# A new order of operations in a five-stage software pipeline of graph layers

## Chip, cores and metric

The kernel runs on one core of a Trainium2 chip. The metric is device time in microseconds (us), the median of several executions; lower is better. The core has five engines that each work through a queue of their own, in order: PE (TensorE, matrix products), DVE (VectorE), ACT (ScalarE), POOL (GpSimd) and SP (SyncE, which here issues all transfers). An instruction that waits holds up everything behind it on its engine.

## What is computed

64 graphs of 256 nodes with 256 features pass through two layers. Each has an adjacency matrix with values that select among four relations.

```
# layer 0: attention of 8 heads, masked by relation r = 0..3
q, k = x @ Wq + bq, x @ Wk + bk                       # per head, 32 columns each
attn = softmax(q k^T / sqrt(32))
out  = sum over r of (attn * (adj == r)) @ (x @ Wv[r] + bv[r])
x1   = layernorm(x + out @ Wo + bo)
x2   = layernorm(x1 + gelu(x1 @ W1 + b1) @ W2 + b2)
# layer 1: two rounds of graph attention, then a feed-forward
Wh = h @ W; e = leaky_relu(Wh a1 + (Wh a2)^T)
h  = softmax(where(adj > 0, e, NEG), axis=1) @ Wh     # done twice
x3 = layernorm(x2 + h)
x4 = layernorm(x3 + relu(x3 @ w_ff1 + b_ff1) @ w_ff2 + b_ff2)
```

All products are in float32.

## The kernel before

Each graph is one chain of 225 named operations. `Graph.operations` (L687) makes them, and the table `PLACES` (L28) gives each a place in time, as if a new graph began every `PERIOD` = 60 units. The launch loop (L769 to L782) makes a list of all operations of all graphs, graph g's shifted by g x 60, sorts it by place, and calls them in that order. A place therefore has no other effect than the order in which instructions enter the five queues. Places go over more than five periods, so while graph g is at its first products, graphs g-1 to g-5 are at later stages. The sort, and no scheduler, fixes the order:

```python
        for _, _, f in sorted(plan, key=lambda p: p[:2]):
            f()
```

Four further functions are sorted in the same way: `v_weights` (L258), two calls of `ffn_weights` (L232) and `gat_weights` (L262), which prepare weights once, at `V_PLACE`, `FFA_PLACE`, `FFB_PLACE` and `GAT_PLACE`; and some fifty loads of weights from `LOAD_PLACE` on, `LOAD_STEP` apart.

The names, with the engine on which they run (m is 0 or 1, a half of the heads; h is 0 to 3, a head):

- load, cast, jT, xT, mask0 to mask4: SP loads x and adj, POOL makes adj bf16, SP transposes it by a transfer, DVE transposes x, POOL compares adj with each relation.
- qk m (PE), qkc m (ACT): queries and keys into PSUM, then into SBUF. s m (PE): scores of four heads. max, rec (DVE), exp, nrm (ACT): softmax.
- eT (DVE), eW, eR (SP): the weights are transposed in squares of 32, written to DRAM and read back in another layout. ec (ACT) copies them to PSUM, pm (DVE) multiplies them with three masks, pl (POOL) with the fourth.
- xS (DVE), vp1 to vp7 (PE), vc1 (ACT), va1 to va9 (DVE), vb0, vb1 (POOL): values of all relations, by seven block products in place of eight, with their sums and bias.
- po m (PE, 32 products of four heads side by side), oT m (ACT copies it to SBUF), y, yb, wo (PE), ya (DVE): head outputs, output product and residual.
- st, rt, nb, ln (DVE, POOL, POOL, ACT), lg, lb (POOL): layer norms 1 to 4.
- For the two feed-forwards (a with GELU, b with ReLU): aT, aW, aR transpose as above; au0 to au3 (PE) the first product; ax0 to ax3 (ACT) its function; aS1 to aS4 (POOL) and ad1 to ad7 (PE) the second product by seven block products; ae, ae1, ae5, ae6, ae7 (DVE) add them; ag, ar (POOL) prepare the residual. The b operations likewise.
- hT, hW, hR, ga0, ga1 (PE), gac0, gac1 (ACT), then twice ip (PE), z (ACT), zm, zx (DVE), ze (ACT), zd (DVE and ACT), with h10, h11 (PE, copied by h1c0, h1c1 on ACT) after the first round (A) and h2 (PE, added by h2a on DVE) after the second (B): graph attention.
- store (SP): the result.

Buffers matter as much as places. Nearly all products of PE (qk, vp, wo, u0 to u3, po, ga, ip, h1, h2, and d2 to d4 together) take turns in two PSUM banks:

```python
    ps_mm = ctx.enter_context(tc.tile_pool(name="ps_mm", bufs=2, space=bass.MemoryType.PSUM))
```

So a product waits until the product two before it has been read by ACT or DVE. d1, d5, d6 and d7 share one more bank; ec has one bank (tag "pe"), the four score tiles one bank each. In SBUF the transposed squares have three buffers, e and pm and pl four, eT three.

ACT computes a function from a set of tables; where the next function is not in the set at hand, an ACT_TABLE_LOAD stands before it in the built program. Exp (exp, ze) and GELU (ax) need different sets.

Of the kernel before, what the change touches and what calls it, by code (L numbers as in the profile page):

```python
# [25 lines left out]

PERIOD = 60.0
PLACES = {  # L28
    "load": 23.357, "xT": 44.608, "cast": 52.922, "jT": 64.605, "mask0": 69.219, "qk0": 72.09,
    "qkc0": 73.299, "mask1": 76.86, "s0": 78.011, "max02": 87.686, "exp02": 89.264, "qk1": 89.326,  # L30
    "max00": 91.141, "qkc1": 92.707, "exp00": 96.206, "rec02": 99.233, "max03": 99.873, "max01": 100.286,
    "mask2": 100.655, "rec00": 100.829, "nrm02": 101.294, "eT02": 101.781, "nrm00": 102.264, "xS": 102.642,
    "eT00": 102.765, "mask3": 102.981, "exp03": 104.45, "exp01": 105.68, "eW02": 108.309, "rec03": 109.52,
    "vp1": 110.158, "rec01": 110.803, "y": 111.209, "vc1": 113.257, "vp6": 114.571, "s1": 115.506,
    "va6": 115.853, "vp2": 116.039, "eR02": 119.674, "nrm01": 120.359, "max10": 120.437, "va1": 120.827,
    "yb": 121.298, "eW00": 123.019, "exp10": 123.155, "max11": 124.031, "nrm03": 124.245, "rec10": 125.086,
    "nrm10": 125.786, "max13": 129.917, "eR00": 129.963, "exp11": 130.688, "vp7": 131.698, "eT01": 131.873,
    "exp13": 132.201, "va7": 132.519, "vb1": 132.554, "eT10": 133.02, "max12": 133.458, "pl00": 133.78,
    "exp12": 134.344, "vp5": 135.541, "eT03": 136.074, "va9": 137.432, "va5": 137.492, "vp4": 138.406,
    "va4": 138.429, "eW03": 139.955, "ec02": 139.991, "eW01": 140.081, "pm02": 140.771, "eR01": 142.073,  # L40
    "rec12": 143.085, "pl02": 143.665, "rec11": 144.369, "rec13": 144.684, "vp3": 145.914, "ec01": 146.17,
    "nrm13": 147.545, "pm01": 149.231, "va3": 149.974, "nrm11": 150.098, "pl01": 150.355, "ec00": 151.68,
    "eR03": 151.833, "nrm12": 153.205, "mask4": 154.895, "eT13": 154.901, "pm00": 156.208, "ec03": 156.841,
    "vb0": 157.326, "eW10": 158.121, "pl03": 159.226, "eT11": 159.823, "pm03": 159.89, "eW13": 159.97,
    "eW11": 161.977, "po0": 162.822, "eR11": 162.889, "ec11": 163.67, "oT0": 164.697, "eR10": 165.613,
    "eR13": 166.702, "pm11": 167.743, "ec13": 167.832, "eT12": 167.88, "pl11": 170.085, "pm13": 170.45,
    "pl13": 172.693, "eW12": 172.935, "pl10": 173.109, "ec10": 174.083, "eR12": 178.038, "pm10": 178.658,
    "ec12": 179.982, "pm12": 181.436, "pl12": 183.147, "po1": 190.604, "oT1": 190.634, "wo": 195.515,
    "ya": 196.954, "st1": 198.358, "rt1": 200.264, "nb1": 202.568, "ln1": 205.212, "aT": 205.925,
    "aW": 214.402, "aR": 215.033, "au0": 217.723, "ag": 219.066, "ax0": 219.075, "au1": 220.077,  # L50
    "au2": 220.423, "ax1": 220.498, "au3": 221.942, "ax2": 222.429, "ax3": 223.227, "aS1": 224.059,
    "aS3": 226.672, "aS2": 228.949, "ad1": 229.288, "ad5": 232.772, "ad7": 233.221, "ar": 236.067,
    "ad6": 237.512, "aS4": 241.549, "ad2": 244.054, "ae5": 244.725, "ad3": 244.935, "ad4": 246.881,
    "ae1": 248.098, "ae6": 248.952, "ae": 249.383, "ae7": 250.355, "st2": 254.869, "rt2": 255.472,
    "nb2": 255.506, "ln2": 255.669, "lg2": 259.788, "lb2": 259.86, "hT": 261.844, "hW": 265.63,
    "hR": 271.783, "ga0": 272.609, "gac0": 274.207, "ga1": 274.252, "gac1": 274.962, "ipA": 275.589,
    "zA": 275.992, "zmA": 277.16, "zxA": 278.103, "zeA": 278.374, "zdA": 283.105, "h10": 283.502,
    "h11": 286.253, "h1c0": 287.71, "h1c1": 289.589, "ipB": 290.919, "zB": 291.939, "zmB": 292.107,
    "zxB": 294.725, "zeB": 295.859, "zdB": 298.561, "h2": 301.635, "h2a": 303.541, "st3": 304.449,
    "rt3": 304.465, "nb3": 307.95, "ln3": 307.966, "bT": 311.255, "bW": 313.954, "bR": 315.237,  # L60
    "bu0": 319.27, "bx0": 320.506, "bu1": 320.552, "bu2": 322.215, "bx1": 323.13, "bu3": 323.143,
    "bx2": 325.826, "bg": 326.199, "bx3": 327.872, "bd1": 328.16, "bS1": 328.916, "br": 329.424,
    "bd5": 330.387, "bS2": 331.057, "bS4": 331.173, "bS3": 331.831, "bd2": 334.692, "be5": 334.871,
    "bd3": 337.158, "bd4": 337.445, "bd6": 337.996, "be": 338.193, "be1": 338.799, "bd7": 340.197,
    "be6": 343.454, "be7": 346.517, "st4": 346.806, "rt4": 355.06, "nb4": 361.434, "ln4": 362.111,
    "lg4": 364.143, "lb4": 369.218, "store": 370.908,
}
LOAD_PLACE, LOAD_STEP = 62.0, 3.0
V_PLACE, FFA_PLACE, GAT_PLACE, FFB_PLACE = 92.0, 199.0, 202.0, 260.0

# [739 lines left out]
```

## Time and profile before

| what | value |
|---|---|
| median of 3 runs | 3690.38 us (3680.24 to 3691.91) |
| the profiled execution | 3687.13 us, span of its instructions 3685.0 us |
| PE, DVE, ACT, POOL busy | 3497.9, 2880.7, 2628.1, 3019.8 us |
| transfers | 458 MB, mean 124 GB/s, 16 engines 42.1% busy |
| first instruction of PE's first product | 7.84 us after the span's start |

The span is from the first to the last instruction of the profile; what the execution takes beyond it is 2.1 us. The transfers are many and of one kind: per graph 11 squares of 256 KB are written and read again. Page lines on them (issues, size, median us from issue to landing):

```profile
eT_d<-eT_sq SPq DMA_DIRECT2D x512, 256.0 KB, 3.1
eT<-eT_d SPq DMA_DIRECT2D x512, 256.0 KB, 3.1
hT_d<-hT_sq SPq DMA_DIRECT2D x64, 256.0 KB, 3.2
```

In the trace a float32 product is two MATMUL records, so qk, of four products, shows as x8. Names of tiles stand for operations: h_ps L664 is h1, h_ps L678 is h2, ga_wps is ga, ffb_ps and ffa_ps are bu and au, ffa_po, ffa_pq, ffb_po and ffb_pq are ad and bd, v_ps is vp, pe L568 is ec.

### The profile page before, as it was taken

The page shows a single profiled execution, that of the slowest core. Times are in us where ns is not written, and L with a number is a line of the kernel's source. Part 1 is how long each engine was busy: PE and PEld are TensorE (multiplying, and loading weights), DVE is VectorE, ACT ScalarE, POOL GpSimd, SP SyncE. Part 2 cuts the span into 40 slices and gives each one's busy share as a digit, 9 for nine tenths or more (in the row PEclk, how much of TensorE's full clock was granted, in tenths as well). Part 3 has the DMA queues.
Part 4 walks back from the last instruction along what each step waited for, and adds up shares of the span by engine and source line. Part 5 has one row for each costly group of instructions (what it writes and reads, how often), then busy time and mean ns, then how long its engine had stood idle before and what let it go on. Part 6 is the DMA issues. An engine that isn't in the chain of part 4 may idle for free.

```text
span 3685.0 us, 73450 instructions
## 1 busy us (share of the span) xinstructions
PE 3497.9 (95%) x25816; PEld 2749.5 (75%) x25816; DVE 2880.7 (78%) x5208; ACT 2628.1 (71%) x6981; POOL 3019.8 (82%) x3142
## 2 busy tenths in 40 slices
PE   6799999999999999999999999999999999999995
PEld 3577777777777777777777777777777777777775
DVE  5688888878888888778788788788788888788762
ACT  4577777777777777777777777777777777777752
POOL 4588888888888888888888888888888888888864
PEclk8899999999999999999999999999999999999997
DMA  6344444444444444444444443444444444444420
GB/s 180 111 119 124 135 126 124 133 118 124 137 124 123 134 126 123 131 127 122 132 127 124 134 128 121 133 127 123 128 126 124 132 126 123 134 127 123 126 86 26
DMA packets 809889, 457.97 MB, mean 124 GB/s; under 512 B 334256, under 2 KB 718896, under 8 KB 809520
## 3 DMA queue, kind: packets, MB, share of 16 engines
q1 hardware_dynamic: 809520, 453.27, 42.1%
q8 instruction: 204, 3.34, 0.4%
q14 instruction: 165, 1.35, 0.1%
HBM read 243.42 MB, written 201.33 MB: 121 GB/s over the span
## 4 chain that ended last, share of the span: by engine, by line
PE 62%; DVE 17%; ACT 8%; DMA 6%; issue 3%; POOL 2%; SPq 2%; POOLq 0%; ACTq 0%; DVEq 0%
PE ffb_ps L387 10%; PE v_ps L511 9%; PE po L589 5%; PE ffa_po L422 5%; DVE pm L572 4%; PE ffb_pq L422 4%; PE qk_ps L487 4%; PE ffa_ps L387 4%; DVE eT_sq L306 4%; PE ffb_po L422 4%; PE ffa_pq L422 3%; PE ga_wps L619 3%; PE s L537 3%; DVE nmax L542 3%; PE h_ps L678 2%
## 5 line engine op out<-in xcount | busy, mean ns | idle before, releaser
L572 DVE TENSOR_TENSOR pm<-rel,pe 128x1536 f32<-128x1536 uint8 x512 | 891.4, 1741 | 123.4 <-ACT pe L568 110.7
L577 POOL TENSOR_TENSOR pl<-rell,eT 128x512 f32<-128x512 bf16 x512 | 595.9, 1170 | 15.5 <-DMA eT<-eT_d 15.2
L560 ACT ACTIVATE e<-e,rden 128x256 f32<-128x256 f32 x1024 | 463.0, 503 | 145.3 <-DVE rden L555 145.1
L387 PE MATMUL ffa_ps<-ffa_T,w 128*128 128x256 f32 x2048 | 478.2, 382 | 8.9 <-ACT e L550 3.3
L550 ACT ACTIVATE e<-s,nmax 128x256 f32<-128x256 f32 x1024 | 475.5, 475 | 5.6 <-DVE nmax L542 4.6
L387 PE MATMUL ffb_ps<-ffb_T,f 128*128 128x256 f32 x2048 | 458.0, 382 | 20.9 <-DMA ffb_T<-ffb_T_d 20.8
L387 PEld LDWEIGHTS ffb_ps<-ffb_T,f 128*128 128x128 f32 x2048 | 392.4, 192 | 102.9 <-issue 36.2
L387 PEld LDWEIGHTS ffa_ps<-ffa_T,w 128*128 128x128 f32 x2048 | 377.1, 192 | 55.3 <-ACT e L550 5.3
L589 PE MATMUL po<-pm,v 128*32 128x256 f32 x6144 | 363.7, 384 | 19.9 <-DVE pm L572 6.6
L568 ACT COPY pe<-eT 128x512 f32<-128x512 f32 x512 | 306.9, 599 | 87.0 <-ACT gb_wh L659 48.0
L306 DVE STREAM_TRANSPOSE eT_sq<-e 128x512 f32<-128x512 f32 x512 | 354.2, 692 | 14.9 <-DMA eT_d<-eT_sq 9.8
L542 DVE TENSOR_REDUCE nmax<-s 128x2 f32<-128x512 f32 x512 | 342.9, 670 | 5.8 <-PE s L537 5.8
L395 ACT ACTIVATE ffb_h<-ffb_ps,bf_c 128x256 f32<-128x256 f32 x512 | 212.4, 466 | 183.2 <-PE ffb_ps L387 183.2
L520 DVE TENSOR_TENSOR v<-v,v_ps 128x512 f32<-128x512 f32 x448 | 298.7, 678 | 35.0 <-PE v_ps L511 32.5
L430 DVE TENSOR_TENSOR ffb_res<-ffb_po,ffb_res 128x256 f32<-128x256 f32 (+2 forms) x256 | 130.4, 509 | 240.7 <-PE ffb_po L422 134.5
L589 PEld LDWEIGHTS po<-pm,v 128*32 128x32 f32 x6144 | 206.8, 110 | 149.1 <-issue 18.2
L479 POOL TENSOR_SCALAR rel<-adT 128x512 uint8<-128x512 bf16 x192 | 289.7, 1509 | 18.8 <-DMA adT<-adb 17.6
L528 POOL TENSOR_TENSOR v<-v,bv_r 128x512 f32<-128x512 f32 (+1 forms) x128 | 232.5, 1816 | 71.5 <-DVE v L520 71.5
L410 POOL TENSOR_TENSOR ffa_h<-ffa_h,ffa_h 128x512 f32<-128x512 f32 x64 | 82.0, 1281 | 221.9 <-ACT ffa_h L395 217.5
L395 ACT ACTIVATE ffa_h<-ffa_ps,b_c 128x256 f32<-128x256 f32 x512 | 212.2, 465 | 36.0 <-PE ffa_ps L387 35.0
L364 ACT ACTIVATE ffa_res<-ffa_res,nb_x,rs_x 128x256 f32<-128x256 f32 x256 | 139.9, 593 | 135.5 <-POOL nb_x L359 135.5
L550 ACT ACTIVATION_READ_ACCUMULATOR e<-s,nmax 128x1 f32 x1024 | 211.1, 206 | 0.0
(154 smaller groups left out, 8444.7 us busy)
## 6 DMA issues: line engine op xcount, KB each, us to landing
eT_d<-eT_sq SPq DMA_DIRECT2D x512, 256.0 KB, 3.1
eT<-eT_d SPq DMA_DIRECT2D x512, 256.0 KB, 3.1
xin<-in_x_dram SPq DMA_DIRECT2D x256, 64.0 KB, 2.7
adi<-in_adj_dram SPq DMA_DIRECT2D x64, 256.0 KB, 3.3
y<-in_x_dram SPq DMA_DIRECT2D x64, 256.0 KB, 4.6
ffa_T_d<-ffa_T_sq SPq DMA_DIRECT2D x64, 256.0 KB, 3.5
ffa_T<-ffa_T_d SPq DMA_DIRECT2D x64, 256.0 KB, 2.9
hT_d<-hT_sq SPq DMA_DIRECT2D x64, 256.0 KB, 3.2
```

Source lines behind the costliest of these rows:

```text
L306: nc.vector.transpose(self.sq.rearrange("p a c k y -> p (c k) a y"), src.rearrange("p c (k a x) -> p (c k) a x", k=KD, a=A))
L387: nc.tensor.matmul(p[:, f - f0, :], self.wa[:, k, f * P:(f + 1) * P], self.x.nodes(k), start=(k == 0), stop=(k == KD - 1))
L395: nc.scalar.activation(self.h[half][:, f1 + f, :], self.ps[f0][:, f, :], self.func, bias=self.ba[:, f0 + f:f0 + f + 1])
L422: nc.tensor.matmul(self.p[bank][:, k], a[:, f], seven[self.name[:3]][i][:, f], start=(f == 0), stop=(f == KF // 2 - 1))
L511: nc.tensor.matmul(self.ps["v", i], a, wv_s[i], start=True, stop=True)
L542: nc.vector.tensor_reduce(self.nmax[m, h], self.s4[m][h].rearrange("p (c n) -> p c n", c=C), AX.X, ALU.max, negate=True)
L550: nc.scalar.activation(e[:, ic, :], self.s4[m][h][:, ic * N:(ic + 1) * N], AF.Exp, bias=self.nmax[m, h][:, ic:ic + 1], accum_out=self.den[ ...
L560: nc.scalar.activation(e[:, ic, :], e[:, ic, :], AF.Copy, scale=self.rden[m, h][:, ic:ic + 1])
L568: nc.scalar.copy(self.pe[m, h], self.et[m, h].t.rearrange("p b c k y -> p (b c k y)"))
L572: nc.vector.tensor_tensor(self.pm[m, h], self.rel.rearrange("p r b c k y -> p r (b c k y)"), bc(self.pe[m, h], [P, R - 1, C * N]), ALU.mult)
L577: nc.gpsimd.tensor_tensor(self.pm_l[m, h], self.rel_l.rearrange("p b c k y -> p (b c k y)"), self.et[m, h].t.rearrange("p b c k y -> p (b ...
L589: nc.tensor.matmul(po[hp, :], self.v[m][:, jc, r, hp], w, start=(r == 0 and jc == 0), stop=(r == R - 1 and jc == C - 1))
```

## The change

Only numbers change: all places in `PLACES`, and the places of the weight preparations and weight loads. `PERIOD`, the functions, the instructions' shapes and the pools stay as they are.

```diff
 PERIOD = 60.0
 PLACES = {
-    "load": 23.357, "xT": 44.608, "cast": 52.922, "jT": 64.605, "mask0": 69.219, "qk0": 72.09,
...
-    "lg4": 364.143, "lb4": 369.218, "store": 370.908,
+    "load": -20.281, "cast": 3.418, "xT": 3.616, "jT": 16.208, "qk0": 32.188, "mask0": 32.245,
...
+    "lg4": 344.387, "lb4": 346.024, "store": 352.412,
 }
-LOAD_PLACE, LOAD_STEP = 62.0, 3.0
-V_PLACE, FFA_PLACE, GAT_PLACE, FFB_PLACE = 92.0, 199.0, 202.0, 260.0
+LOAD_PLACE, LOAD_STEP = 20.0, 3.0
+V_PLACE, FFA_PLACE, GAT_PLACE, FFB_PLACE = 50.0, 168.0, 198.0, 235.0
```

What it makes of the queues is seen when all places are taken modulo 60 from qk0 of graph g. A number after the name tells how many graphs back the operation belongs (qk0 is of graph g, bu0-4 of graph g-4). PE's queue over one period before:

```
qk0 wo-2 vp5-1 s0 vp4-1 bu0-4 bu1-4 bu2-4 bu3-4 vp3-1 bd1-4 qk1 bd5-4 ga0-3 ga1-3 bd2-4 ipA-3
bd3-4 bd4-4 au0-2 bd6-4 au1-2 bd7-4 au2-2 au3-2 po0-1 h10-3 h11-3 ad1-2 vp1 ipB-3 ad5-2 ad7-2
vp6 s1 vp2 ad6-2 h2-3 ad2-2 ad3-2 ad4-2 po1-1 vp7
```

and after:

```
qk0 vp5-1 ad5-3 ad2-3 ad6-3 ad4-3 ad3-3 vp4-1 vp2-1 s0 vp3-1 qk1 bu0-4 bu1-4 bu2-4 bu3-4 au0-2
au1-2 bd1-4 po0-1 ga0-3 ga1-3 bd5-4 ipA-3 vp1 bd6-4 vp6 bd2-4 bd4-4 bd3-4 au2-2 bd7-4 h10-3 s1
h11-3 au3-2 ipB-3 ad1-2 po1-1 vp7 wo-1 h2-3 ad7-2
```

After, in the same period, the parts of the other queues that the prediction follows:

```
DVE  st1-2 rec11-1 ae7-3 va9-1 va5-1 ae5-3 bT-4 rec13-1 ae6-3 rec12-1 rec10-1 ae-3 st2-3 va4-1 va1-1
     aT-2 eT11-1 va3-1 pm03-1 eT13-1 max00 max01 pm01-1 hT-3 max03 rec00 pm02-1 eT12-1 max02 xS ...
     pm12-1 max10 max11 max13 eT02 eT03 zmB-3 zxB-3 st4-4 max12 va7 zdB-3 pm00 ya-1 ae1-2 h2a-3 st3-3
ACT  exp12-1 qkc0 ln3-4 exp13-1 ln4-5 nrm11-1 ln1-2 nrm10-1 ec03-1 nrm12-1 nrm13-1 ln2-3 qkc1 bx0-4
     ec01-1 bx1-4 exp00 bx2-4 exp01 bx3-4 ec02-1 ax0-2 nrm00 ax1-2 ec13-1 exp03 oT0-1 gac0-3 gac1-3
     exp02 zA-3 vc1 ec11-1 nrm01 zeA-3 zdA-3 ec10-1 ax2-2 h1c0-3 ec12-1 nrm03 h1c1-3 nrm02 ax3-2
     zB-3 exp11 ec00 oT1-1 zeB-3 zdB-3 exp10
SP   load+1 eR01-1 eW02-1 bW-4 bR-4 aW-2 aR-2 store-5 eR02-1 eW13-1 eW11-1 eR13-1 hW-3 hR-3 eR11-1
     eW12-1 eW10-1 eR10-1 eR12-1 eW00 eR00 jT+1 eW01 y eW03 eR03
```

In the queues before, ACT has ax0 to ax3 with nrm02, nrm00 and zdA between them and no Exp; SP has bW, bR, two eW, eR01, load, then hW and hR next to each other.

## The prediction

> **What bounds the kernel now.** I read the page first (busy shares and slices), then the busy time by windows, then who PE waited for in the middle of the run, then the timeline around PE's one regular wait, and last the chain of waits at both ends.
>
> ```profile
> PE 3497.9 (95%) x25816; PEld 2749.5 (75%) x25816; DVE 2880.7 (78%) x5208; ACT 2628.1 (71%) x6981; POOL 3019.8 (82%) x3142
> PE   6799999999999999999999999999999999999995
> ```
> PE is full from the third slice to the last but one. Only there can an order gain or lose.
>
> ```profile
> 1000.00:1600.00 600.00, 585.56 (x4378) 460.92 (x4377) 488.39 (x887) 445.22 (x1187) 511.93 (x535) 1.00 0.43 127
> 1600.00:2200.00 600.00, 585.14 (x4393) 461.51 (x4392) 487.58 (x886) 443.98 (x1184) 512.21 (x533) 1.00 0.43 127
> ```
> Windows: after the length come the busy times of PE, PEld, DVE, ACT, POOL, then clock and DMA. PE idles 14.7 us in 600, the clock is full, and no other engine is above 86%. Who ends PE's idle time between 1000 and 3400 us (total, times, longest):
>
> ```profile
> PE h_ps L664 <- ACT oT L595: 40.1, 44, 1.4
> PE ga_wps L619 <- DMA hT<-hT_d: 10.1, 12, 2.7
> PE ffa_ps L387 <- DMA ffa_T<-ffa_T_d: 3.2, 4, 1.6
> ```
> So one wait comes in each of the 44 periods, of 0.9 us; the transfer hT adds 10.1/44 = 0.23 us. The timeline shows the first:
>
> ```profile
> 2443.97 0.59 ACT L568 COPY pe<-eT 128x512 f32<-128x512 f32 x1
> 2444.58 1.28 ACT L550 ACT_TABLE_LOAD   x1
> 2445.87 0.48 ACT L550 ACTIVATE e<-s,nmax 128x256 f32<-128x256 f32 x1
> 2446.79 0.37 ACT L595 COPY oT<-po 128x256 f32<-128x256 f32 x1
> 2447.21 1.14 PE L664 MATMUL h_ps<-ga_wh,ga_z 128*128 128x258 f32 x4 [1.21 <-ACT oT L595]
> ```
> h11 needs the second of two PSUM buffers, which oT0 empties. oT0 stands on ACT behind ec11, a table load and exp03. From the chain of waits at both ends:
>
> ```profile
> 203.34 1.73 PE qk_ps L487 x8
> ...
> 3460.07 1.73 PE qk_ps L487 x8
> ```
> These are qk0 of graphs 4 and 63, so a full period is (3460.07-203.34)/59 = 55.2 us; 203.3 us lie ahead and 3685.0-3460.1 = 224.9 behind.
>
> [...] I use start-to-start times. [...] the load starts 0.02 us after ec11's end and exp03 0.01 us after the load, so I charge 1.28 us. [...] Here like transfers of 256 KB land in 2.0 us (ffb_T_d) to 3.5 us (ffa_T_d)[...].
>
> **The change, part by part.** No computation comes or goes; each engine's queue is reordered.
>
> *Table loads.* GELU (ax0 to ax3) and Exp are different sets.
>
> ```profile
> L395 ACT ACT_TABLE_LOAD x64 | 82.1, 1283 | 0.3
> L550 ACT ACT_TABLE_LOAD x62 | 79.5, 1283 | 1.1
> ```
> Before, the four GELUs stand together: one pair of loads a graph. After, the queue reads ax0, ax1, exp03, exp02, zeA, ax2, ax3, exp11: two pairs. The built program has 257 loads for 129, so ACT does 128 x 1.283 = 164 us more and reaches 2792 us, 76%. It costs only where ACT's queue sets PE; checked below.
>
> *PE.* Start-to-start times of before without a wait: 12 products of 1.73 (qk, up-products u, wo, h2) 20.8; 7 vp of 0.86, 6.0; 14 down-products d of 0.89, 12.5; 2 po of 3.59, 7.2; 2 s, 2.2; ga, h1 and ip, 4.1; and 0.1 on each side of each s and po, 0.8. Sum 53.5 us. Before pays 55.2: 1.0 at h11, 0.4 at ga0, 0.3 elsewhere.
>
> Next I laid the new PE queue out back to back, qk0 at 0, and followed what each PE step needs through the other queues, with the trace's steps: DVE 0.60 (pm 1.67), ACT 0.73 for pairs reading PSUM, 0.81 nrm, 0.91 exp, 0.52 ec, 1.0 ln, POOL 1.23 (pl 1.12, mask 1.46), 0.05 a hand-over. The tight places, in order of the period:
>
> 1. vp2 (7.90) takes the bank that ae empties after ad3 (6.15): 6.15+1.05+0.05+0.55+0.05 = 7.85. Free, by nothing. In front of ae stands bT, behind ln3 (ends 3.75), so DVE is there in time (6.0).
> 2. bu0 (12.62) takes vp3's bank, behind ae, st2, va4, va1, aT, eT11, va3: 11.8. Its data: bT ends 4.5, bW and bR 2.2 and 2.7: about 10. Free.
> 3. po0 (23.99) needs pm02: bu3 ends 19.70, bx3 20.5, ec02 21.0, pm02 22.8. pl02 follows vb0 on POOL (18.9+1.1). Free.
> 4. ga1 (28.56) takes po0's bank. ACT from bu3's end: bx3, ec02, load, ax0, nrm00, ax1, ec13, load, exp03 end at 27.3; po0 ends 27.65, oT0 28.1. Both loads are in this chain, with 1.0 us to spare before ga1. This is before's wait: gone, because ga0 and bd1 lie between.
> 5. ga0 (27.58) needs hT. aT ends 10.5; aW 3.5 lands 14.1; SP, which stops at aR until then, issues aR, store, eR02, eW13, eW11 in 2.4 us. eR13 stops SP until eW13 lands, near 20[...]; then hW 3.1, hR 3.8: near 27.2. By the transfers' extremes 26 to 29. Cost -0 to 1.4, and I take 0.3: before loses as much there.
> 6. po1 (44.59) takes au3's bank, 41.65+1.89+0.04+0.82+0.05 = 44.45; ax2's load falls ahead of au3's end. Free by 0.1.
> 7. h2 (50.87) needs zdB. On DVE zdB stands behind va7, which waits for vp7 (48.18): 48.18+1.12+0.04+0.59+1.11+0.05 = 51.1. Cost 0.2. exp11's load is ahead of oT1 (47.2 against po1's end 48.25): hidden.
>
> Everything else (buffers of e, eT, pm, pl, squares) comes free over 0.5 us before a PE step needs it, by the same steps. Waits known: 0.3+0.2. For those my steps don't see, 0.2 (before too has 0.3 elsewhere). New period 54.2 us, gain 1.0.
>
> *SP and POOL.* Same issues, new places: eR00 now follows eW00 at once and stops SP about 3 us, in front of jT and eW01; jT's first reader mask0 comes 12 us after it lands, and eT01 is ready later than the stop ends. store moves ahead of eR02; its operand lb4 is done at 11.5, so it doesn't stop SP, where before it waited for POOL. POOL adds nothing and has some 6 us free a period.
>
> *Ends.* Head: the same first products and the same weights; gat_weights moves from 10 to 46 us into period 2, out of ffn_weights' neighbourhood. I keep 203.3, +-8. Tail: bu0 stands 12.6 instead of 6.4 us after qk0, which delays the last graph's last feed-forward: 225+6 = 231, +-8.
>
> Sum: 203.3 + 59 x 54.2 + 231 = 3632 of span. The profiled execution took 3687.13, 2.1 above its span: 3634. The median shown, 3690.38, is 3.3 above that execution, inside the runs' spread of 11.7; I add 2 of it: 3636, so 438 + 59 x T for every case.
>
> **Rivals.**
>
> *One wait for another (no change).* Places 1, 6 and 7 have 0.2 us or less to spare. If my 0.04 to 0.05 hand-overs are short, as for before, whose h11 wait flips between 0.39 and 1.2, three waits of 0.4 arise on top of the known 0.5: T = 55.0, 438+59x55.0 = 3683. For it: the 0.3 us a period in before that no list names. Against: PE-bound waits in series aren't added, since a later PE step relaxes the next place.
>
> *The burst on SP (slower).* Place 5: ad3 to hT by way of ae, aT, aW, aR, store, eR02, eW13, eR13, hW, hR, five of them stopping SP in turn. PE work between ad3 and ga0 is 21.4 us, the chain 21.0. Before has no such run there: hW goes out at 10.6, hR at 14.0 with nothing between them, hT lands at 17.8 against ga0 at 17.7, and still 0.2 is lost. If transfers in the burst land 0.5 us later each than I took, the chain is 23.5, T = 53.5+2.1+0.4 = 56.0, total 3742. It decides where T passes (3690-438)/59 = 55.1, a chain of 22.6. For it: DMA is busy 43% and y, in a burst, takes 4.6 us. Against: hT's typical 3.8 us is charged already.
>
> *Table loads show (slower).* If ec02 waits for eR02 (lands near 19, needed 20.5) by 2.5 us, place 4 loses 1.5 and po0 1.2: T about 55.6, 3718.
>
> **How the numbers follow.** This kernel's measurement tells 0.3% (11 us) from no change. Forecast (T 53.6 to 54.85): 0.66, from 438+59x53.6 = 3600 to 3674, 3636 likeliest. Waits exchanged: 0.12, 3674 to 3701, of which 0.02 still faster by over 11 us. Burst 0.15, 3701 to 3765. Table loads 0.07, 3701 to 3730. Faster by over 0.3% 0.68, within 0.10, slower 0.22. The range 3592 to 3720 leaves out about 0.12 above and 0.03 below, where head or tail also gain their 8 us.
>
> **What would show it.** PE's wait "h_ps L664 <- ACT oT" vanishes; a wait of "h_ps L678 <- ACT gb_wh" of 0.2 us comes; table loads x128 and near x124 under L395 and L550, 1283 ns each; ACT near 2790 us; start-to-start of qk0 54.2. Wrong if PE waits over 1 us a period at ga_wps for hT, at v_ps for DVE, or at ffb_ps or po for ACT, or if head and tail move by over 15 us.

## The result, and the profile after

The changed kernel takes 3914.07 us (median of 4 runs, 3906.63 to 3951.67), the kernel before in the same comparison 3688.23. The ratio is 1.0636 (95% interval 1.0566 to 1.0706): 226 us slower, where 3636 was forecast, and beyond the range's upper end of 3720. The profiled execution took 3914.44 us, its span is 3912.5 us.

From the page of the changed kernel, busy times and slices:

```profile
PE 3565.3 (91%) x25816; PEld 2758.2 (70%) x25816; DVE 3131.6 (80%) x5208; ACT 2799.4 (72%) x7109; POOL 3012.4 (77%) x3142
PE   5899989999999899998999999899999899999985
```

PE now has holes in the middle of the run. DVE has as many instructions as before and is busy for 251 us more. ACT has 128 instructions more, the table loads, and its 2799 us are near the 2792 of the sum. A window of the changed kernel (busy times of PE, PEld, DVE, ACT, POOL, then clock, DMA share and GB/s):

```profile
1000.00:1600.00 600.00, 558.62 (x4079) 434.42 (x4079) 499.50 (x825) 443.25 (x1130) 478.75 (x498) 0.98 0.41 119
```

PE idles 41.4 us in 600, nearly three times as much as before, and no engine looks full. Who ends its idle time from 1000 to 3400 us (total, times, longest):

```profile
PE ffb_po L422 <- DVE rden L555: 112.3, 41, 5.8
PE v_ps L511 <- DVE ffa_res L430: 40.6, 41, 1.0
PE ga_wps L619 <- DMA hT<-hT_d: 2.6, 4, 1.0
```

Before's wait of h11 (h_ps L664) for oT is gone, as forecast, and the transfer hT costs 2.6/41 = 0.06 us a period. Two new waits came, one each in every period. The second is vp2 waiting for ae, place 1 of the prediction. The first is bd6 (ffb_po), on no list of mine.

From qk0 to qk0 the periods are of two lengths: of 50 in the middle of the run, 30 take 56.2 us and 20 take 63.0 in the mean. The mean from graph 4 to graph 63 is 58.82. Set against the sum:

| part | forecast | traced | difference |
|---|---|---|---|
| head, to qk0 of graph 4 | 203.3 | 198.4 | -4.9 |
| 59 periods | 59 x 54.2 | 59 x 58.82 | +272.6 |
| tail | 231 | 243.7 | +12.7 |
| span | 3632 | 3912.5 | +280 |

So the period is the place to look. Start to start, PE's steps in the new order take what the sum gave them, but for two: from vp4 to vp2 it is 2.1 us instead of 0.86, and from vp1 to bd6 2.2 in the short periods (1.3 lost), 6.8 in the long ones (5.9 lost). Here is PE's timeline in a long period (start, duration, then the idle time ahead and who ended it):

```profile
1234.52 1.02 PE L511 MATMUL v_ps<-wv,xT 128*128 128x512 f32 x2
1241.29 2.05 PE L422 MATMUL ffb_po<-f_t,ffb_t 128*128 128x128 f32 x8 [5.75 <-DVE rden L555]
1243.13 1.91 PE L511 MATMUL v_ps<-wv_t,xs 128*128 128x512 f32 x2
```

After the wait, bd6 takes 1.84 us to the next start and vp6 1.71, where 0.97 and 0.86 are usual, and the granted clock of this stretch and of the next is low (windows of the changed kernel):

```profile
1236.40:1241.50 5.10, 0.21 (x1) 0.24 (x2) 5.10 (x11) 3.21 (x10) 2.12 (x2) 0.67 0.21 70
1241.50:1243.00 1.50, 1.50 (x8) 1.50 (x9) 1.09 (x2) 0.73 (x3) 0.00 (x0) 0.50 1.12 346
```

Around the wait of 1.14 us in a short period the clock stays at 1.00 (1593.00 to 1594.50 and 1594.50 to 1597.00 us), and in the 5.75 us wait it falls to the 0.50 of the second window; from 1245.00 to 1247.00 us it is 1.00 again. From 1000 to 3400 us bd6 takes 2.04 or 2.05 us after each of the 15 waits of 5.32 to 5.76 us, and 1.02 to 1.13 after the 26 of 0.49 to 1.17 us. The slower steps behind it cost about 2.2 us more: the long periods are 6.8 us longer than the short ones, and the longer wait accounts for 4.6 of them (6.8 less 2.2). In the first window DVE is busy all the time, 5.10 of 5.10. Whoever is late is DVE, and it isn't waiting by the look of it. The chain of waits of the changed kernel through this stretch says with what (start, us, what):

```profile
1228.03 8.29 DVE xs L453
...
1240.56 0.59 DVE ffb_res L430
1241.15 0.08 DVE rden L555
...
1241.29 2.05 PE ffb_po L422 x8
```

bd6 waits for be1 (ffb_res L430; the list names rden, which ends last, but the experiment with be1 late shows that it is be1), and be1 stands behind one 128x128 difference of xS that took 8.3 us. In each of the 41 periods between 1000 and 3400 us, short or long, bd6 starts 4.25 us after xS ends: it is late by as much as xS is. DVE's and POOL's timelines of the changed kernel there:

```profile
1227.96 8.36 DVE L453 TENSOR_TENSOR xs<-xT 128x128 f32<-128x128 f32 x1
1236.35 0.29 DVE L453 TENSOR_TENSOR xs<-xT,xs 128x128 f32<-128x128 f32 x1
```

```profile
1227.80 1.29 POOL L410 TENSOR_TENSOR ffb_t<-ffb_h,ffb_t 128x512 f32<-128x512 f32 x1
...
1233.31 2.29 POOL L577 TENSOR_TENSOR pl<-rell,eT 128x512 f32<-128x512 bf16 x2
1235.55 2.97 POOL L479 TENSOR_SCALAR rel<-adT 128x512 uint8<-128x512 bf16 x2
```

Between the first and the last of these POOL works without a gap. The difference is done only when POOL has come to its masks (L479); the next one, beside the masks, takes 0.29. In a short period the same four differences look like this (DVE, then POOL):

```profile
1585.84 1.28 DVE L453 TENSOR_TENSOR xs<-xT 128x128 f32<-128x128 f32 x1
1587.15 1.25 DVE L453 TENSOR_TENSOR xs<-xT,xs 128x128 f32<-128x128 f32 x1
1588.33 1.37 DVE L453 TENSOR_TENSOR xs<-xT 128x128 f32<-128x128 f32 x1
1589.62 0.69 DVE L453 TENSOR_TENSOR xs<-xT,xs 128x128 f32<-128x128 f32 x1
```

```profile
1585.65 1.32 POOL L410 TENSOR_TENSOR ffb_t<-ffb_h,ffb_t 128x512 f32<-128x512 f32 x1
1586.88 1.37 POOL L331 TENSOR_TENSOR ffa_res<-y,g_r 128x512 f32<-128x512 f32 x1
1588.22 1.33 POOL L410 TENSOR_TENSOR ffb_t<-ffb_h,ffb_t 128x512 f32<-128x512 f32 x1
1589.50 0.66 POOL L457 CAST adb<-adi 128x512 bf16<-128x512 int32 x1
```

Each DVE record ends 0.15 us after a POOL record does: 1587.12 and 1586.97, 1588.40 and 1588.25, 1589.70 and 1589.55, 1590.31 and 1590.16. Here DVE gets one difference done at each boundary of POOL's run, in 1.25 to 1.37 us each for the first three. The long one took 8.36, in which six boundaries passed, and in the masks, which read SBUF too, the differences took 0.28 to 0.29. In a period xS is DVE's only TENSOR_TENSOR with both inputs in SBUF: pm, ya, va and the additions take one input from PSUM. zm, a COPY_PREDICATED which reads a mask and a constant column from SBUF, takes 0.76 to 0.78 us in the changed kernel from 1000 to 3400 us, whether POOL works beside it or not.

Before, xS stood where POOL mostly had gaps: of its 176 differences between 1000 and 3400 us, 143 began with POOL idle and took 0.25 to 0.29 us; the other 33 took 0.36 to 1.11. By form, before and then after (busy, mean ns; table loads with it):

```profile
L453 DVE TENSOR_TENSOR xs<-xT 128x128 f32<-128x128 f32 x128 | 64.6, 505 | 0.0
L453 DVE TENSOR_TENSOR xs<-xT,xs 128x128 f32<-128x128 f32 x128 | 36.9, 288 | 2.2
```

```profile
L453 DVE TENSOR_TENSOR xs<-xT 128x128 f32<-128x128 f32 x128 | 300.4, 2347 | 0.0
L395 ACT ACT_TABLE_LOAD x128 | 164.2, 1283 | 62.3 <-PE ffa_ps L387 61.1
L550 ACT ACT_TABLE_LOAD x124 | 159.1, 1283 | 2.2
L453 DVE TENSOR_TENSOR xs<-xT,xs 128x128 f32<-128x128 f32 x128 | 90.2, 705 | 2.2
```

xS goes from 101.5 us in all to 390.6, that is from 1.6 to 6.1 us a graph. The 289 us are more than DVE's whole rise of 251.

The other wait, vp2's, has another cause. DVE's timeline of the changed kernel ahead of it:

```profile
1560.64 0.69 DVE L430 TENSOR_TENSOR ffa_res<-ffa_po,ffa_res 128x512 f32<-128x512 f32 x1 [1.40 <-PE ffa_po L422]
...
1565.89 0.42 DVE L430 TENSOR_TENSOR ffa_res<-ffa_po,ffa_res 128x256 f32<-128x256 f32 x1 [2.05 <-PE ffa_po L422]
...
1569.06 0.56 DVE L430 TENSOR_TENSOR ffa_res<-ffa_pq,ffa_res 128x384 f32<-128x384 f32 x1
```

These are ae1, ae7 and ae of one graph. ae1 adds d1, a product of before po1, but it starts when ad7 ends (1560.53); ae7 adds d7, finished at that same 1560.53, but it starts when ad6 ends (1565.85). d1, d5, d6 and d7 are columns of one tile in one PSUM bank, and each addition here starts 0.11 and 0.04 us after the end of a later product that PE has been given ahead of it on that tile. Likewise bd6 waits for be1, though they touch different columns. No run here tells whether the shared bank or the shared tile makes the program wait. What stands on DVE between ae7 and ae (va9, va5, ae5, bT and others) is held back with it, ae ends at 1569.62, and vp2 follows (PE's timeline of the changed kernel):

```profile
1567.56 1.12 PE L511 MATMUL v_ps<-wv,xs 128*128 128x512 f32 x2
1569.67 1.13 PE L511 MATMUL v_ps<-wv,xT 128*128 128x512 f32 x2 [0.99 <-DVE ffa_res L430]
```

Adding up with weights 0.6 and 0.4 for short and long periods: PE's work 53.5, vp2 1.25, bd6 0.6 x 1.3 + 0.4 x (5.9 + 2.2) = 4.0, ga0 0.1: 58.9, against the traced 58.82.

### The profile page after: what moved, and what is told of

Read it like the earlier page. It is cut to its first block, busy times and chain, and to the rows that moved or that the text cites. A ratio compares the mean times of both kernels' runs of the same rounds, so it can differ in the third digit from the quotient of the medians.

```text
span 3912.5 us, 74077 instructions
## 1 busy us (share of the span) xinstructions
PE 3565.3 (91%) x25816; PEld 2758.2 (70%) x25816; DVE 3131.6 (80%) x5208; ACT 2799.4 (72%) x7109; POOL 3012.4 (77%) x3142
## 4 chain that ended last, share of the span: by engine, by line
PE 71%; DVE 19%; ACT 4%; issue 3%; DMA 2%; SPq 1%; POOL 0%; POOLq 0%; DVEq 0%; ACTq 0%
PE po L589 9%; PE ffb_ps L387 9%; PE ffa_ps L387 9%; PE v_ps L511 8%; PE ffa_po L422 6%; DVE xs L453 5%; PE qk_ps L487 5%; PE ffb_po L422 5%; PE ffb_pq L422 5%; PE s L537 3%; DVE pm L572 3%; PE h_ps L664 3%; PE h_ps L678 3%; DVE ffa_res L430 3%; PE wo_ps L609 3%
## 5 line engine op out<-in xcount | busy, mean ns | idle before, releaser
L387 PEld LDWEIGHTS ffa_ps<-ffa_T,w 128*128 128x128 f32 x2048 | 385.2, 191 | 51.5 <-ACT v L523 1.1
L306 DVE STREAM_TRANSPOSE eT_sq<-e 128x512 f32<-128x512 f32 x512 | 343.4, 690 | 6.4 <-DMA eT_d<-eT_sq 6.1
L542 DVE TENSOR_REDUCE nmax<-s 128x2 f32<-128x512 f32 x512 | 325.5, 665 | 0.0
L422 PE MATMUL ffb_po<-f_t,ffb_t 128*128 128x128 f32 x1024 | 161.7, 308 | 176.9 <-DVE rden L555 173.8
L410 POOL TENSOR_TENSOR ffa_t<-ffa_h,ffa_t 128x512 f32<-128x512 f32 x128 | 163.8, 1280 | 197.6 <-ACT ffa_h L395 197.6
L430 DVE TENSOR_TENSOR ffa_res<-ffa_po,ffa_res 128x256 f32<-128x256 f32 (+2 forms) x256 | 132.5, 518 | 222.4 <-PE ffa_po L422 220.6
L422 PEld LDWEIGHTS ffb_po<-f_t,ffb_t 128*128 128x128 f32 x1024 | 148.6, 217 | 229.2 <-issue 158.0
L589 PEld LDWEIGHTS po<-pm,v 128*32 128x32 f32 x6144 | 190.0, 111 | 159.8 <-DVE pm L572 14.2
L410 POOL TENSOR_TENSOR ffa_t<-ffa_h 128x512 f32<-128x512 f32 x64 | 81.6, 1275 | 285.6 <-ACT ga_wh L659 147.8
L453 DVE TENSOR_TENSOR xs<-xT 128x128 f32<-128x128 f32 x128 | 300.4, 2347 | 0.0
L479 POOL TENSOR_SCALAR rel<-adT 128x512 uint8<-128x512 bf16 x192 | 286.8, 1504 | 8.4 <-DMA adT<-adb 8.4
```

Source lines behind the costliest of these rows:

```text
L306: nc.vector.transpose(self.sq.rearrange("p a c k y -> p (c k) a y"), src.rearrange("p c (k a x) -> p (c k) a x", k=KD, a=A))
L387: nc.tensor.matmul(p[:, f - f0, :], self.wa[:, k, f * P:(f + 1) * P], self.x.nodes(k), start=(k == 0), stop=(k == KD - 1))
L422: nc.tensor.matmul(self.p[bank][:, k], a[:, f], seven[self.name[:3]][i][:, f], start=(f == 0), stop=(f == KF // 2 - 1))
L453: nc.vector.tensor_tensor(o, t, u, ALU.subtract)
L542: nc.vector.tensor_reduce(self.nmax[m, h], self.s4[m][h].rearrange("p (c n) -> p c n", c=C), AX.X, ALU.max, negate=True)
L589: nc.tensor.matmul(po[hp, :], self.v[m][:, jc, r, hp], w, start=(r == 0 and jc == 0), stop=(r == R - 1 and jc == C - 1))
```

## Experiments

The expectations name three theories. A: xS's waits for POOL make DVE late, and that makes bd6 late. B: it is DVE's order and amount of work at that place, with xS as ordinary work. C: it is ACT with its 128 further table loads. Periods are means from graph 4 to graph 63 of each profiled execution; a ratio is to the kernel before, run beside it (3680.59 us for the first four, 3676.62 for the next four, 3679.23 for the last).

| kernel | median us | ratio (95%) | period |
|---|---|---|---|
| changed kernel, xS on POOL | 3673.79 | 0.9985 (0.9978 to 0.9991) | 54.91 |
| changed kernel, xS with one input | 3674.71 | 0.9985 (0.9978 to 0.9992) | 54.91 |
| changed kernel, ae1, ae7, ae5 late | 3827.50 | 1.0422 (1.0363 to 1.0480) | 58.2 |
| kernel before, xS among POOL's work | 3627.39 | 0.9859 (0.9841 to 0.9876) | 54.08 |
| changed kernel, xS on POOL and ae late | 3617.12 | 0.9835 (0.9820 to 0.9850) | 54.03 |
| the same with ReLU for GELU | 3605.96 | 0.9806 (0.9791 to 0.9820) | 53.99 |
| kernel before, xS on POOL | 3625.63 | 0.9856 (0.9840 to 0.9873) | 54.16 |
| kernel before with ReLU for GELU | 3608.62 | 0.9811 (0.9796 to 0.9826) | 54.01 |
| changed kernel, be1, be6, be5 late | 3773.68 | 1.0248 (1.0229 to 1.0268) | 56.63 |

### xS without its waits: on POOL, or with one input

In the changed kernel, all else the same, the four differences go to POOL, in the same place:

```diff
-                nc.vector.tensor_tensor(o, t, u, ALU.subtract)
+                nc.gpsimd.tensor_tensor(o, t, u, ALU.subtract)
```

> The kernel after with xS (four differences of 128x128) issued on POOL instead of DVE, at the same place. Theory A[...]: DVE's xS, with both inputs in SBUF, waits for POOL's running operations; that makes be1 late on DVE and bd6 late on PE, by 1.2 us in most periods and 5.9 plus 2 us of slower PE clock in the others. Then the records of xS under L453 stay below 0.6 us, PE's wait at ffb_po is gone, the period falls from 58.7 to 54.9 us (53.5 of PE work, 1.25 at vp2, 0.1 at ga0), the total to 442+59x54.9 = 3681 us. Theory B (queue): DVE's queue ahead of be1 is simply too long in this order; moving 1.3 us of work off it takes back 1.3 us a period in place of 3.8, total about 3835. Theory C (table loads): the 128 added loads on ACT are what costs; no change, 3910.

In the second, DVE writes the same four tiles in the same place from one input each; the differences themselves are left out:

```diff
-                nc.vector.tensor_tensor(o, t, u, ALU.subtract)
+                nc.vector.transpose(o, t)
```

> The kernel after with the four differences of xS replaced by four transposes of 128x128 with one input, on DVE at the same place (leaves out the differences, so four of the seven value products get other data). Queue, place and waits stay; only the second SBUF input goes. Theory A[...]: each record about 0.3 us, period 54.9, total 3681. Theory B (queue or a semaphore wait shown as busy time): records of 1.3 and 8.3 us stay, total about 3910. Theory C: 3910.

Measured: 3673.79 and 3674.71 us, 7 and 6 us from what A gave. By form, the second kernel's row (all four differences are now of one form):

```profile
L453 DVE STREAM_TRANSPOSE xs<-xT 128x128 f32<-128x128 f32 x256 | 55.8, 276 | 0.0
```

With one input the same place on DVE costs 276 ns a record, and 239 us of the time go. DVE has as many instructions in the same order as in the changed kernel, so B falls, and C's table loads are untouched, so C falls: it is the second input, A. A transpose is another operation than a difference, too; that DVE's two-input operation isn't slow as such is seen by va, which takes one input from PSUM and 678 ns in the mean both in this order and in the old one. Of PE's waits in the kernel with xS on POOL, one regular one is left:

```profile
PE v_ps L511 <- DVE ffa_res L430: 43.5, 44, 1.0
```

bd6's wait has vanished whole; vp2's stays as it was, 1.0 each time. So vp2's wait doesn't come from xS.

### The addition that waits for a later product

ae1, ae7 and ae5 get places just ahead of ae6, so that bT, va9 and va5 no longer stand behind them:

```diff
-    "ae1": 211.793, ... "ae7": 218.694,
-    "ae5": 219.904,
+    "ae1": 220.44, ... "ae7": 220.45,
+    "ae5": 220.46,
```

> The kernel after with ae1, ae7, ae5 moved behind bT and rec13 on DVE, next to ae6 (places 220.44 to 220.46). Theory: ae1 waits for ad7 and ae7 for ad6[...] and that delays h2a, st3, va9, bT and ae, on which vp2 waits 1.25 us each period. Then PE's wait at v_ps vanishes and the period falls by 1.25 to 57.5: total about 3838. Rival: ae is late for another reason (ln3 through POOL's rt3 and nb3); the wait at v_ps stays, 3910.

Measured: 3827.50 us (3813.79 to 3865.79), 11 us from 3838 and 87 below the changed kernel. Its PE waits:

```profile
PE ffb_po L422 <- DVE rden L555: 134.1, 41, 5.8
PE v_ps L511 <- DVE ffa_res L430: 12.6, 41, 0.3
```

vp2's wait falls from 1.0 to 0.3 us a period and the short periods from 56.2 to 55.26. The bd6 wait is larger than in the changed kernel, since 23 of 50 periods of this profiled execution were long ones, against 20. It is also the slowest of the four (3865.79), which is why its period is 58.2 where 57.5 was expected. That the share of long periods changes from run to run is the likely reason why this kernel's runs differ by 52 us and those with xS on POOL by 11: the mean granted clock falls from 0.971 in the fastest run to 0.963 in the slowest, as more long waits would have it, but the other runs have no trace.

### Both, and the table loads

xS on POOL and the late additions together:

> The kernel after with both edits: xS on POOL, and ae1, ae7, ae5 moved behind bT and rec13. Theory: the two waits are in series on PE and add, so the 0.95 us that ae_late saved at vp2 comes off 54.9 as well: period 53.9, of which 53.5 is PE's work, total about 430+59x53.9 = 3610. Rival: with PE faster, another queue (POOL, now 85% busy, or a transfer) becomes late and gives it back: 54.5 or more, 3645 or more.

Measured: 3617.12 us, 7 from the expectation. Head 196.6, period 54.03, tail 232.4. Its window (columns as above):

```profile
1000.00:1600.00 600.00, 595.57 (x4485) 466.13 (x4478) 484.56 (x859) 483.86 (x1234) 539.06 (x588) 1.00 0.44 130
```

PE idles 4.4 us in 600; what is left of vp2's wait is 0.3 us each time. This is what the order gives when the two causes are out: the forecast period was 54.2. It is the best complete version here, 59.5 us below the kernel before. To it, ReLU for GELU, which leaves out the function and with it all but one of the 257 table loads:

```diff
-            self.ffa = Ffn(w1, b1_c, AF.Gelu, w2, g1_r, b2_r, f"ffa{g}")
+            self.ffa = Ffn(w1, b1_c, AF.Relu, w2, g1_r, b2_r, f"ffa{g}")
```

> xs_ae with ReLU in the place of GELU (leaves out GELU in the first feed-forward): no function set changes, so all but one of the 257 table loads go, 329 us of ACT's work. Theory: in this order they are hidden behind PE; the time stays within 12 us of xs_ae, nearly all of that from the two ends. Rival C: table loads show on PE; 0.5 us or more a period, so 30 us or more faster than xs_ae.

Measured: 3605.96, 11 us less. The period is 53.99 against 54.03; the gain lies in the head (190.8 against 196.6) and the tail (225.8 against 232.4), where PE isn't full. In the full periods four table loads a graph, 5.1 us of ACT, are hidden.

### Only half of the wait: be1 late

In the changed kernel xS stays on DVE as it is, and be1, be6 and be5 get places behind be, so that bd6 no longer waits for an addition behind xS:

```diff
-    "be1": 304.422, ... "be6": 309.955, ... "be5": 312.24,
+    "be1": 314.12, ... "be6": 314.14, ... "be5": 314.16,
```

> The kernel after with be1, be6, be5 moved on DVE behind pm10, in front of be7 (places 314.12 to 314.16); xS stays on DVE[...]. Theory: bd6 waits for be1[...], and be1 stands behind xS; with be1 moved, bd6 no longer waits. The DVE work behind xS is then late for other PE steps (va6 for au2, zdA and be for h10) by less: short periods 55.0 in place of 56.2, long ones about 59 in place of 62.9, total about 3780. Rival: bd6 waits for its data (bS2 on POOL) or for something else ahead of xS: no change, 3910.

Measured: 3773.68 us, 6 from 3780. The PE waits:

```profile
PE v_ps L511 <- ACT ga_z L638: 51.6, 17, 3.1
PE v_ps L511 <- DVE ffa_res L430: 41.5, 42, 1.0
```

bd6 doesn't wait any more, although xS's records are nearly as long as in the changed kernel (2274 ns in the mean for the first kind, against 2347). Short periods take 54.82, long ones 59.6. The lateness of DVE then shows at vp6, 17 times and by 3 us each (51.6 / 17), in the long periods: on ACT exp02 waits for a transpose eT that stands behind xS on DVE (3.75 us in one period), zA stands behind exp02, and vp6 takes the bank that zA empties. That is another place than the expectation named. vp2's wait is unchanged. So xS's waits for POOL make DVE late, and the order on the shared tile decides where and how dearly it is paid: 140 us (3914.07 - 3773.68) hang on be1's place, 100 (3773.68 - 3673.79) remain without it.

### The kernel before, with xS in POOL's way

The opposite test: in the kernel before, xS moves to where POOL works without gaps.

```diff
-"xS": 102.642,
+"xS": 91.2,
```

> The kernel before with one place changed: xS from 102.642 to 91.2, behind max00, where POOL runs bS1 to vb0 without a gap. Theory A: xS takes 5 us or up to 8 us there in place of 1.7, pm00 and rec02 come late, and po0 and the ACT queue with them: period up by 2 to 6 us, total 3800 to 4040. Theory B: xS is 1.3 us of ready work put earlier, total 3690 within 15.

Measured: 3627.39 us. Both theories were wrong, A also in sign. By form of this kernel:

```profile
L453 DVE TENSOR_TENSOR xs<-xT,xs 128x128 f32<-128x128 f32 x128 | 162.0, 1266 | 2.2
L453 DVE TENSOR_TENSOR xs<-xT 128x128 f32<-128x128 f32 x128 | 77.8, 608 | 0.0
```

xS did become longer, 239.8 us in all against 101.5, as A said. But the kernel became 53 us faster. Its PE waits:

```profile
PE ga_wps L619 <- DMA hT<-hT_d: 4.8, 9, 1.5
PE ga_wps L619 <- DVE xs L453: 2.8, 5, 0.7
PE h_ps L664 <- ACT oT L595: 0.8, 2, 0.6
```

h11's wait for oT, 40.1 us in before, is nearly gone. The chain of waits of the kernel before, in the period that the prediction shows, says why:

```profile
2440.01 1.00 DVE xs L453
...
2442.36 0.06 DVE ga_rden L657
...
2442.44 0.79 ACT ga_wh L659 x2
...
2447.21 1.14 PE h_ps L664 x4
```

xS stands on DVE ahead of eT00 and zdA (ga_rden, ga_wh), and ACT's ax3, ec11, table load, exp03 and oT0 come behind zdA. In 43 of 44 periods between 1000 and 3400 us h11 starts 5.5 us after xS ends. Where the first difference took 0.25 us (11 periods) h11 waited about 0.4; where it took 1.05 or more, it waited about 1.2. So xS's waits for POOL, though short, were part of before's own regular wait. At the new place one kind of record takes 1266 ns in the mean instead of 288, and yet PE waits for xS only 5 times, 2.8 us in all. The last two kernels test this: the kernel before with xS on POOL (the edit of the first experiment), and with ReLU (the edit above), which takes the table load out of the same chain.

> The kernel before with xS on POOL at its old place. b_xs_burst was 53 us faster than before, where I had expected it slower[...]. Then taking xS off DVE also ends the wait at h11: total 3620 to 3640. Rival: b_xs_burst gained because other operations got earlier, not because of xS; then b_pool stays at 3680 within 12.

> The kernel before with ReLU in the place of GELU (leaves out GELU): 128 table loads of 1.283 us go. The same chain to h11 holds one table load. Theory: without it oT0 comes 1.28 us earlier and the wait at h11 of 0.9 us ends: 3620 to 3640. Rival: the chain is set elsewhere (oT0 waits for po0 alone), 3680 within 12.

Measured: 3625.63 and 3608.62 us, the first inside its expected span, the second 11 below, with periods of 54.16 and 54.01. Of the wait of h11 the first kernel keeps 0.7 us, once, and the second none.

Moving xS, taking it off DVE, or taking the load away each end it. The old order with xS on POOL is 8.5 us above the new order with both edits. The runs of the two don't overlap (3622.52 to 3627.30 and 3614.32 to 3618.55), but the intervals of their ratios overlap by a thousandth, so that little is shown for the new order beyond the old one once xS is out of POOL's way.

## Why the prediction was wrong

**The step that failed first: the price of xS.** All of DVE's work but pm was charged at 0.60 us a step; for xS's four small differences that is 2.4 at most, and they take 4.5 in a short period and 9.1 in a long one. Here the step that failed is a term of the sum, and its size depends on another engine. I followed every DVE instruction through its own queue and never laid it beside POOL's. That a DVE instruction can wait for POOL's records within its own busy time, as xS does, was on no list, and "everything else comes free over 0.5 us" was claimed by steps that had no such term. Before's own row showed a sign: 505 ns for xs<-xT against 288 for the same size of xs<-xT,xs. The same cost was in before's h11 wait, which the prediction saw flip between 0.39 and 1.2 and put down to hand-overs. Taking xS away from the path is worth 240 us (3914.07 to 3673.79), which is shown by two kernels that do it in different ways.

**The second: place 1, "Free, by nothing".** The sum had ae start when ad3 and bT allow it, at 7.25 us. It starts at 8.7 (1569.06 - 1560.37, qk0's start), because ae1 and ae7 wait for later products on their PSUM tile and hold bT and va9 behind them. I had the sharing in the description of the buffers, and used it for no step. This was 1.25 us a period; the edit took 87 us from the changed kernel and 57 from the one with xS on POOL.

**bd6 itself.** It was not among the seven tight places. Its wait for be1 is again that for a shared tile, and it turned xS's lateness into most of the loss, 140 of 240 us.

**What held.** PE's start-to-start sum of 53.5: the kernel with both edits runs at 54.03 with 0.3 of wait left. h11's wait vanished. Place 4, the table loads hidden behind PE, is shown by ReLU: 0.04 us a period. Place 5, the burst on SP, cost 0.06 us, and 0.03 with both edits (1.2 / 45), where 0.3 was charged and the rival had 2.1: the rival of the transfers falls, and so does that of the table loads. Places 2, 3, 6 and 7 cost nothing that the list of waits shows; the 0.2 for h2 didn't come. The head was 4.9 us shorter than taken, the tail 12.7 longer; 6 of these go with xS (237.3 on POOL), and with both edits it is 232.4 against 231.

**Why the range failed too.** Every rival was a wait that I had found and sized. "PE waits over 1 us a period at v_ps for DVE" stands among the signs that would make the forecast wrong, and it came, 1.0 by the list of waits and 1.25 from start to start; but no case priced DVE as a whole being late, by a cost that depends on what runs on another engine. And the gain of 1.0 us a period that the forecast saw, by ga0 and bd1 between oT0 and h11, needs no new order: h11's wait hung in part on xS, and one place changed in the kernel before ends it (3627.39).

**What stays open.** Why the first difference ends at POOL's next boundary in three periods of five and only after six boundaries in the others, and by what means it waits for POOL at all: the runs show when it ends, and that a transpose with one input in its place doesn't wait (302 ns at most). The long ones all began 0.15 to 0.18 us after the start of a POOL record, but so did most of the short ones. In the two kernels in the old order in which it began 0.33 us or more after that start, or with POOL idle, none was long; that is a hint, and no run tests it. Not tried: the four differences in fewer instructions, and the new order with xS on DVE in a gap of POOL's.

## What to carry to other kernels

An order can't be judged engine by engine: for a DVE TENSOR_TENSOR with two SBUF inputs, as xS is, look at what POOL does at that time (1.6 us a graph in one place, 6.1 in another), and give it another engine (240 us less in the new order; 51 in the old one, 3676.62 - 3625.63), or a place where nothing behind it leads to the bound engine (53 us less in the old one); a PSUM input, as va has, at 678 ns in both orders, was not tried for it. When products share a PSUM tile, write down which addition waits for which product by the tile as well as by the data, before trusting a slack of some tenths of a us. A longer busy time at an unchanged count of instructions was here a wait that the list of waits doesn't show; the mean duration by form does.

## What was not expected of the hardware

- A 128x128 DVE difference with two SBUF inputs takes 0.25 to 0.29 us with POOL idle (143 of them in the kernel before), 1.25 to 1.37 in most cases beside POOL's unbroken run of additions, products and the cast, 0.69 beside the cast (changed kernel, 1585.84 to 1590.31 us), and 8.34 to 8.39 in the 15 cases from 1000 to 3400 us where it lets six boundaries between these pass. A transpose with one input takes 276 ns in the same place (the kernel with one input).
- POOL's masks (TENSOR_SCALAR, bf16 to uint8), though they read SBUF too, don't hold it up: of the changed kernel's differences from 1000 to 3400 us, 45 lie within a mask record, and each took 0.28 to 0.29 us.
- The same difference on POOL takes 458 to 461 ns in the median (changed kernel, xS on POOL), so that moving xS to POOL costs it about 1.8 us a graph, which its slack took.
- In the changed kernel the wait of 5.75 us that ends at 1241.29 leaves PE's granted clock at 0.50 and adds about 2.2 us behind itself; the wait of 1.14 us that ends at 1594.56 leaves it at 1.00, and bd6 behind it takes 1.13 us.
